# Turning rows by DMA instead of on TensorE, and a gated unit's new state in three GpSimd operations

## The chip, the cores and the metric

The kernel runs on one core of a Trainium2 chip. The metric is the device time of one execution in microseconds (us). The kernel before took 2233.61 us, the median of three runs (2232.93 to 2242.04).

The core's engines run side by side, each through its own queue in order, and wait for one another through semaphores: PE (TensorE, the matrix unit), DVE (VectorE), ACT (ScalarE), POOL (GpSimd) and SP, which here only issues DMAs. GpSimd issues DMAs too. SBUF is the on-chip memory of 128 partitions; PSUM is the smaller memory into which PE writes.[...]

## The reference

There are 16 graphs of 1024 nodes with 128 features each and a dense 0/1 adjacency matrix. Layer 0 runs four steps of a gated unit over each graph, layer 1 thins the adjacency matrix row by row ("skipping" below) and runs three graph layers over the thinned one. Cut to what matters here:

```python
# layer 0, four times, h = x at first
hw = h @ weight[i];  m = adj.T @ hw
gx = m @ w_ih.T + b_ih;  gh = h @ w_hh.T + b_hh
r = sigmoid(xr + hr);  z = sigmoid(xz + hz);  n = tanh(xn + r * hn)
h = (1 - z) * n + z * h

# layer 1, skipping: for each row n in order
num = row.sum();  sf = (num + 1) // 2 if num > 10 else 1
rm = row & (cumsum(row) % sf == 0)          # only if num > 1 and the node counts
carry[n] = row & ~rm                        # the row loses these entries ...
carry[:, n] = carry[:, n] & ~rm             # ... and so does column n of all rows
```

What row n removes, entry j, is also taken from row j at column n. So a later row needs, of every earlier row, the entry at its own place: a column of what the earlier rows left, which has to be turned into a row.

## The kernel before

The kernel has two stages. In the first, the gated unit (class Gated) and the skipping (class FixPoint) run together; in the second (class Sage), the three graph layers. A slower general path follows under a condition that the inputs don't meet.

**The gated unit.** Two streams take the graphs in turn, so that a layer of one stream runs while the other's state is turned and prepared. There are 64 layers of this kind (16 graphs, four steps), and each treats its 1024 nodes in two halves f of 512 columns. The state h of a stream is one SBUF tile of 128 features by 1024 nodes (`st.ht`). In `layer`, L1096 multiplies with the adjacency matrix, L1108 is every gate matmul, L1118 the sigmoid of r, L1121 and L1123 add the parts of n on DVE, L1124 is the tanh (written into the tile r) and L1127 the sigmoid of z. Then the new state is made as z * h - (z - 1) * n: L1131 (first half) or L1135 (second half) makes z * h on GpSimd, L1136 makes (z - 1) * n on DVE, and L1137 subtracts on GpSimd. The loop of L1133 does this for both halves after the gates of both. In the very last layer DVE does GpSimd's part too. Reading the new state begins a layer later, when the other stream's gates run: `turn` (L1041) turns one half after the other.

**The skipping.** A block is 128 rows, number k of a graph, for four graphs g at once; 32 blocks follow each other, k from 0 to 7 for graphs 0 to 3, then for 4 to 7, and so on. A block first masks its rows with what earlier blocks left: `read_back` (L715) reads, for k of 2 and more, the columns of this block from all blocks but the last one, out of DRAM (`not_r`, profile name e_nr), one DMA per graph on SP's queue, into one of four buffers f_rt; the part from the last block is still in SBUF (`fresh`, f_nr). `turn` (L726) transposes each 128x128 square on PE into one PSUM bank (`tr`, f_tr), `keep` (L731) masks the rows from there in one DVE operation over 128k columns, and `count` (L739) is a scan along the rows. Then the removals inside the block are settled, and `rows` (L870, L872) makes what is left of each row and stores it with L873. `check` of the gated unit (L1992) looks over a tile h_test that SP loads (L998).

**The order.** In this stage every engine's order is that of the program. `steps` is a generator with a yield between pieces; `layer` calls `aside(n)` at ten places, and each takes one piece, so a block of the skipping goes with exactly two layers of the gated unit. The masks of graphs 0 to 3 stand at places 6 and 8 of one layer and 2 and 4 of the next; `rows` at 2 to 4 of a block's later layer; the reads for the next block are issued at place 3, between the third and the fourth mask. The DMA queue of SP holds, in order, the four stores of L873, the four reads of L715 and the load of h_test. A read may start when its buffer is free and the stores it reads from have landed.

Of the kernel before, what the change touches and what calls it, by code (L numbers as in the profile page):

```python
# [8 lines left out]
F32 = mybir.dt.float32  # L9
BF = mybir.dt.bfloat16  # L10
# [4 lines left out]
AF = mybir.ActivationFunctionType  # L15
ALU = mybir.AluOpType
# [5 lines left out]
P = 128  # L22
B = 16
N = 1024
C = 128
NB = N // P
HF = 512
L0 = 4
# [602 lines left out]
class FixPoint:  # L631
# [76 lines left out]
    def read_back(self, i, g):  # L708

        if i >= len(self.todo) or self.todo[i][0] < 2:  # L710
            return
        k, b0 = self.todo[i]
        k1 = k - 1
        rt = self.rts.tile([P, NB - 2, P], BF, name="f_rt")
        self.nc.sync.dma_start(rt[:, :k1, :], self.not_r[b0 + g, :k1 * P, k * P:k * P + P]  # L715
                               .rearrange("(j p) n -> p j n", p=P))
        self.left[i, g] = rt

    def turn(self, i, g):

        k = self.todo[i][0]
        if k:
            rt = self.left.pop((i, g), None)
            for j in range(k):
                src = rt[:, j, :] if j < k - 1 else self.fresh[g][:, k * P:k * P + P]
                self.nc.tensor.transpose(self.tr[:, j, :], src, self.cst["ident_b"])  # L726

    def keep(self, i, a):
        k = self.todo[i][0]
        if k:  # L730
            self.nc.vector.scalar_tensor_tensor(a[:, :k * P], self.tr[:, :k, :].rearrange("p k n -> p (k n)"),  # L731
                                                0.0, a[:, :k * P], op0=ALU.is_ge, op1=ALU.mult)

    def count(self, i, g, a, rank, other):
        nc = self.nc
# [6 lines left out]
    def steps(self):  # L742

        nc, G = self.nc, self.G
        for c in range(G):
            self.load(c)
        old = None
        for i, (k, b0) in enumerate(self.todo):
            diag = slice(k * P, k * P + P)

            yield
            if old:
                old.settle()
                old.wide_u(0)
            yield
            if old:
                old.wide_u(1)
                old.rows(0)
            yield
            if old:  # L760
                old.wide_u(2)
                old.rows(1)
            yield
            if old:
                old.rows(2)
                old.wide_u(3)
                old.rows(3)
            a = [self.loaded.pop((i, g)) for g in range(G)]
            pt = self.ps.tile([P, G, P], F32, name="f_pd")
            turned = pt.rearrange("p g n -> p (g n)").bitcast(BF)[:, :G * P].rearrange("p (g n) -> p g n", g=G)  # L770
            for g in range(G):
                nc.tensor.transpose(turned[:, g, :], a[g][:, diag], self.cst["ident_b"])
            yield
            if old:
                old.last_u()

            both = self.small.tile([P, G, P], BF, name="f_both")
            for g in range(G):
                nc.vector.tensor_mul(both[:, g, :], a[g][:, diag], turned[:, g, :])
            nc.gpsimd.affine_select(both, both, pattern=[[0, G], [1, P]], compare_op=ALU.is_gt, fill=0.0,  # L780
                                    base=0, channel_multiplier=-1)
            self.turn(i, 0)
            yield
            rank = self.two.tile([P, G, N], F16, name="f_rank")
            self.keep(i, a[0])
            self.count(i, 0, a[0], rank, pt)
            yield
            yield
            self.turn(i, 1)
            self.keep(i, a[1])  # L790
            yield
            self.count(i, 1, a[1], rank, pt)
            if i == 0:

                for c in range(G, self.LOTS):
                    self.load(c)
            yield
            yield
            yield
            self.turn(i, 2)  # L800
            self.keep(i, a[2])
            self.count(i, 2, a[2], rank, pt)
            yield
            for g in range(G):
                self.read_back(i + 1, g)
            yield
            self.turn(i, 3)
            self.keep(i, a[3])
            self.count(i, 3, a[3], rank, pt)

            num = self.sm[:, 0, 0, :]
            nc.vector.tensor_scalar(num, rank[:, :, N - 1], 1.0, None, op0=ALU.mult)
            q = self.params(num, 0)
            u = self.diag_u(rank[:, :, diag], q)
            if old:
                old.check()
                for g in range(G):
                    self.load(G * (i - 1) + g + self.LOTS)
            yield
            x = self.removed(u, q, both)  # L820
            yield
            yield
            pd, num = self.less(x, rank, 1)
            rd = self.small.tile([P, G, P], F16, name="f_rd")
            q = self.params(num, 1, lambda: nc.vector.tensor_sub(rd, rank[:, :, diag], pd))
            u = self.diag_u(rd, q)
            yield
            x = self.removed(u, q, both)
            yield
            old = self.Block(self, i, a, rank, both, x)  # L830
            yield
        yield
        old.settle()
        for n in range(4):
            old.wide_u(n)
            if n < 3:
                yield
            old.rows(n)
        yield
        old.last_u()  # L840
        yield
        old.check()
# [81 lines left out]
class Gated:  # L924
# [7 lines left out]
    def __init__(self, ctx, tc, cst, x, adj, weight, w_ih, w_hh, b_ih, b_hh, summed, bad):  # L932
        self.tc, self.nc, self.cst = tc, tc.nc, cst
        self.x, self.adj, self.summed, self.bad = x, adj, summed, bad
        nc = self.nc
        pool = lambda name, **k: ctx.enter_context(tc.tile_pool(name=name, **k))
        self.adjp = pool("h_adj", bufs=NB)
        self.one = pool("h_one", bufs=1)
        self.wk = pool("h_wk", bufs=2)

        self.ps6 = pool("h_ps6", bufs=6, space=PSUM)
        self.wi = self.one.tile([C, L0, 3, C], F32, name="h_wi")
        self.wh = self.one.tile([C, L0, 3, C], F32, name="h_wh")
        self.bi = self.one.tile([C, L0 * 3], F32, name="h_bi")
        self.bh = self.one.tile([C, L0 * 3], F32, name="h_bh")
        self.bs = self.one.tile([C, L0 * 3], F32, name="h_bs")
        self.given = weight, w_ih, w_hh, b_ih, b_hh

    def bank(self):
# [20 lines left out]
    def prepare(self):  # L970
        nc, ident = self.nc, self.cst["ident"]
# [17 lines left out]
        for t, dst in zip(self.b_in, (self.bi, self.bh)):  # L989
            pt = bank()  # L990
            nc.tensor.transpose(pt[:, :L0 * 3], t, ident[:L0 * 3, :L0 * 3])
            nc.vector.tensor_copy(dst, pt[:, :L0 * 3])
        nc.vector.tensor_add(self.bs, self.bi, self.bh)

    def load_test(self, n):
        if n < B * 2:
# [81 lines left out]
    def layer(self, st, l, aside):  # L1078

        nc, wk = self.nc, self.wk  # L1080

        aid = nc.vector if (st.b, l) == (B - 1, L0 - 1) else nc.gpsimd
# [19 lines left out]
        bias = lambda t, g: t[:, 3 * l + g:3 * l + g + 1]  # L1102
# [5 lines left out]
                nc.tensor.matmul(pg, lhs, rhs, start=(i == 0), stop=(i == len(mm) - 1))  # L1108
            return pg

        rest = []
        for f in range(2):
            h, m = st.ht[:, half[f]], ms[f]
            r = wk.tile([C, HF], F32, name="h_r")
            z = wk.tile([C, HF], F32, name="h_z")
            zh = wk.tile([C, HF], F32, name="h_zh")
            pr = gate((w(self.wh, 0), h), (w(self.wi, 0), m))
            nc.scalar.activation(r, pr, AF.Sigmoid, bias=bias(self.bs, 0))  # L1118
            aside(5 + 2 * f)
            ph = gate((w(self.wh, 2), h))  # L1120
            nc.vector.scalar_tensor_tensor(r, ph, bias(self.bh, 2), r, op0=ALU.add, op1=ALU.mult)  # L1121
            px = gate((w(self.wi, 2), m))
            nc.vector.tensor_add(r, px, r)  # L1123
            nc.scalar.activation(r, r, AF.Tanh, bias=bias(self.bi, 2))  # L1124
            aside("rest" if f == 0 else 8)
            pz = gate((w(self.wh, 1), h), (w(self.wi, 1), m))
            nc.scalar.activation(z, pz, AF.Sigmoid, bias=bias(self.bs, 1))  # L1127

            rest.append((r, z, zh, h))
            if f == 0:  # L1130
                aid.tensor_tensor(zh, z, h, ALU.mult)  # L1131
                aside(6)
        for f, (r, z, zh, h) in enumerate(rest):  # L1133
            if f == 1:
                aid.tensor_tensor(zh, z, h, ALU.mult)  # L1135
            nc.vector.scalar_tensor_tensor(r, z, 1.0, r, op0=ALU.subtract, op1=ALU.mult)  # L1136
            aid.tensor_tensor(h, zh, r, ALU.subtract)  # L1137
        aside(9)

    def run(self, steps):  # L1140
# [937 lines left out]
```

## Time and profile before

| what | before |
|---|---|
| median of three runs | 2233.61 us |
| profiled execution, whole | 2232.83 us |
| its span, first to last instruction | 2230.8 us |
| PE, DVE, ACT, POOL busy | 2129.7, 1926.9, 1327.2, 1082.6 us |
| joint stage (about 40 to 1310 us), from 40 to 1270 us: PE, DVE, POOL busy | 1223.90, 1156.59, 596.79 of 1230 us |
| L726, transposes of f_rt and of f_nr | 336 and 112 |
| L731, masks | 112 |
| L1136 on DVE | 128, 99.1 us |
| L1131, L1135, L1137 on POOL | 63, 63 and 126; 80.1, 81.3 and 205.3 us |

Rows of the profile name line, engine, operation, written tile "<-" read tiles, shapes and how many; then busy time and mean, or, in order of time, the start and the length in us. "PEld" is the load of a matmul's stationary operand, which overlaps matmuls. The end of a matmul is modelled, so for PE the distance between starts tells more than the length. Bracketed text is idle time of the engine and what ended it.

### The profile page before, as it was taken

What the parts mean: (1) busy time and instruction counts of PE and PEld (TensorE: products, weight loads), DVE (VectorE), ACT (ScalarE), POOL (GpSimd) and SP (SyncE); (2) the same over time, 40 slices, a digit from 0 to 9 for tenths busy, and PEclk for the clock granted to TensorE, in tenths of its full rate; (3) what the DMA queues carried; (4) which work ended last, traced back from release to release, by engine and by line L of the source; (5) the groups of instructions that cost most, each with busy time, mean ns of one, the idle gap of its engine ahead of it and who ended that gap; (6) DMA issues with size and microseconds to landing.
All of it is one profiled execution on the core that took longest, in us unless ns stands there. A gap on an engine that the chain in (4) does not pass through costs nothing. (4 is left out here: it accounts for less than half of the span.)

```text
span 2230.8 us, 33341 instructions
## 1 busy us (share of the span) xinstructions
PE 2129.7 (95%) x10665; PEld 1456.6 (65%) x10665; DVE 1926.9 (86%) x4338; ACT 1327.2 (59%) x3238; POOL 1082.6 (49%) x1092
## 2 busy tenths in 40 slices
PE   6999999999999999999999979999999899998987
PEld 4566655666656666555665557777777678887865
DVE  4999999999998999999999978888888766666877
ACT  3657557565565656556566465666666455556756
POOL 4347437356355364364463346777777344551002
PEclk9999999999999999999999989999999999999989
DMA  8247347347356265364383259888888577765404
GB/s 251 71 103 240 80 114 229 71 120 214 86 156 177 73 200 138 90 201 118 73 264 85 64 184 329 305 305 297 305 301 304 169 259 260 257 221 174 152 29 144
DMA packets 214396, 402.46 MB, mean 180 GB/s; under 512 B 59586, under 2 KB 80740, under 8 KB 214212
## 3 DMA queue, kind: packets, MB, share of 16 engines
q1 hardware_dynamic: 168388, 280.68, 37.3%
q0 software_dynamic: 41472, 117.46, 19.3%
q10 hardware_dynamic: 4352, 2.11, 0.4%
q8 instruction: 86, 1.41, 0.3%
q14 instruction: 98, 0.80, 0.1%
HBM read 324.49 MB, written 109.25 MB: 194 GB/s over the span
## 5 line engine op out<-in xcount | busy, mean ns | idle before, releaser
L1108 PE MATMUL h_g<-h_h,h_wh 128*128 128x512 f32 x768 | 399.2, 601 | 3.1 <-DVE h_r L1121 3.1
L1108 PE MATMUL h_g<-h_ms,h_wi 128*128 128x512 f32 x768 | 392.1, 592 | 0.0
L739 DVE TENSOR_TENSOR_SCAN f_rank<-f_a,f_first,f_pd 128x1024 f16<-128x1024 bf16 x128 | 299.2, 2343 | 3.3
L1137 POOL TENSOR_TENSOR h_h<-h_zh,h_r 128x512 f32<-128x512 f32 x126 | 205.3, 1629 | 195.2 <-DVE h_r L1136 172.2
L1096 PE MATMUL h_g<-h_a,h_hi 128*128 128x512 f32 x1024 | 282.8, 417 | 2.2 <-DMA h_a<-in_adj_dram 2.0
L1108 PEld LDWEIGHTS h_g<-h_ms,h_wi 128*128 128x128 f32 x768 | 145.6, 190 | 183.9 <-issue 166.8
L1096 PE MATMUL h_g<-h_a,h_lo 128*128 128x512 f32 x1024 | 264.1, 395 | 0.0
L1513 POOL CAST p_b<-p_at 128x512 uint8<-128x512 f32 x256 | 219.4, 879 | 84.2 <-DVE p_at L1505 59.8
L1096 PEld LDWEIGHTS h_g<-h_a,h_hi 128*128 128x128 f32 x1024 | 188.4, 188 | 63.8 <-issue 20.1
L1096 PEld LDWEIGHTS h_g<-h_a,h_lo 128*128 128x128 f32 x1024 | 190.0, 188 | 39.4
L1406 ACT ACTIVATE s_junk<-s_o 128x128 bf16<-128x128 f32 x384 | 114.0, 298 | 170.7 <-DVE s_o L1399 170.7
L1131 POOL TENSOR_TENSOR h_zh<-h_z,h_h 128x512 f32<-128x512 f32 x63 | 80.1, 1271 | 275.5 <-ACT h_z L1127 275.5
L1108 PEld LDWEIGHTS h_g<-h_h,h_wh 128*128 128x128 f32 x768 | 129.2, 190 | 85.9 <-issue 65.5
L1099 ACT COPY h_ms<-h_g 128x512 f32<-128x512 f32 x128 | 73.8, 577 | 183.3 <-PE h_g L1096 139.3
L1124 ACT ACTIVATE h_r<-h_r,h_bi 128x512 f32<-128x512 f32 x128 | 92.3, 721 | 131.2 <-DVE h_r L1123 131.1
L916 ACT ACTIVATE f_u<-f_rank,f_q 128x128 f16<-128x128 f16 (+7 forms) x128 | 110.6, 867 | 74.9 <-DVE f_rank L856 74.9
L1992 DVE SCALAR_TENSOR_TENSOR p_junk<-p_a 128x1024 bf16<-128x1024 f32 x96 | 125.7, 1309 | 0.0
L893 ACT ACTIVATE f_pd<-f_rank,f_q 128x128 f32<-128x128 f16 x128 | 59.1, 461 | 109.8 <-DVE f_q L701 106.6
L1781 PE MATMUL q_ob<-s_wxp,q_xt 128*128 128x256 f32 x512 | 123.4, 385 | 0.3
L1505 DVE SCALAR_TENSOR_TENSOR p_at<-p_nr,p_u 128x128 fp32r<-128x128 bf16 (+1 forms) x192 | 102.5, 543 | 20.5 <-ACT p_at L1497 15.0
L1492 PE MATMUL p_u<-ident_b,p_nr 128*128 128x128 bf16 x1024 | 97.2, 224 | 7.2 <-DVE p_at L1505 5.0
L1423 POOL TENSOR_TENSOR q_rl<-s_r,q_rh 128x512 fp32r<-128x512 f32 x32 | 41.1, 1285 | 128.0 <-ACT q_rh L1422 105.5
(260 smaller groups left out, 4946.3 us busy)
## 6 DMA issues: line engine op xcount, KB each, us to landing
h_a<-in_adj_dram POOLq DMA_DIRECT2D x128, 512.0 KB, 9.5
p_a<-in_adj_dram SPq DMA_DIRECT2D x96, 512.0 KB
f_a<-in_adj_dram POOLq DMA_DIRECT2D x128, 256.0 KB, 6.6
e_nr<-f_nr SPq DMA_DIRECT2D x128, 256.0 KB
p_nr<-e_nr SPq DMA_DIRECT2D x32, 1024.0 KB
h_test<-in_adj_dram SPq DMA_DIRECT2D x32, 512.0 KB
s_at<-p_b SPq DMA_DIRECT2D x32, 512.0 KB
s_ag<-s_ag SPq DMA_DIRECT2D x64, 256.0 KB
```

The costliest lines, as they stand in the source:

```text
L739: nc.vector.tensor_tensor_scan(out, a, other[:, 0, 0:1].to_broadcast([P, N]), start, op0=ALU.add, op1=ALU.bypass)
L916: nc.scalar.activation(u[:, :n1], rank[:, g, :n1], AF.Abs, bias=q[:, 1, g:g + 1], scale=q[:, 0, g:g + 1])
L1096: nc.tensor.matmul(pm[f], part[:, j, :], st.adj[j][:, half[f]], start=(j == 0 and n == 0), stop=(j == NB - 1 and n == 1))
L1108: nc.tensor.matmul(pg, lhs, rhs, start=(i == 0), stop=(i == len(mm) - 1))
L1124: nc.scalar.activation(r, r, AF.Tanh, bias=bias(self.bi, 2))
L1137: aid.tensor_tensor(h, zh, r, ALU.subtract)
L1406: self.nc.scalar.activation(junk, o[:, i, :], AF.Square, accum_out=ss[:, i:i + 1])
L1492: nc.tensor.matmul(pu[:, i * P:(i + 1) * P], v[:, 4 * f + i, j * P:(j + 1) * P], self.cst["ident_b"], start=True, stop=True)
L1505: self.nc.vector.scalar_tensor_tensor(g["at"][:, j, c0:c0 + low], v[:, j, c0:c0 + low], 0.0, pu[:, :low], op0=ALU.is_lt, op1=ALU.is_lt)
L1513: self.nc.gpsimd.tensor_copy(g["b", f][:, j, :], g["at"][:, j, f * HF:(f + 1) * HF].bitcast(F32))
L1781: nc.tensor.matmul(pb[:, i], g["xt"][:, f, blk], self.wxp, start=(i % 2 == 0), stop=False)
L1992: nc.vector.scalar_tensor_tensor(junk, a, 0.0, a, op0=ALU.is_gt, op1=ALU.not_equal, accum_out=bad[:, c:c + 1])
```

## The change

Two things change. The columns of older rows are read from DRAM by a DMA that transposes them on the way, so that PE turns only the square from the last block; the mask is then two DVE operations where k is over 1, one on the DMA's tile in SBUF and one on PE's square in PSUM, and each graph g has its own square of `tr`. And the new state is h + (1 - z) * (n - h): ACT gives 1 - z as the sigmoid of the negated sum (a scale of -1 and a negated bias, made once by a small DVE operation), and GpSimd does a subtraction, a product and a sum, for each half right after that half's gates; DVE's L1136 goes. In the last layer DVE does these three.

```diff
 def read_back(self, i, g):
-        rt = self.rts.tile([P, NB - 2, P], BF, name="f_rt")
-        self.nc.sync.dma_start(rt[:, :k1, :], self.not_r[b0 + g, :k1 * P, k * P:k * P + P]
-                               .rearrange("(j p) n -> p j n", p=P))
+        rt = self.rts.tile([P, (NB - 2) * P], BF, name="f_rt")
+        self.nc.sync.dma_start(rt[:, :k1 * P], self.not_r[b0 + g, :k1 * P, k * P:k * P + P], transpose=True)
         self.left[i, g] = rt

     def turn(self, i, g):
         k = self.todo[i][0]
         if k:
-            rt = self.left.pop((i, g), None)
-            for j in range(k):
-                src = rt[:, j, :] if j < k - 1 else self.fresh[g][:, k * P:k * P + P]
-                self.nc.tensor.transpose(self.tr[:, j, :], src, self.cst["ident_b"])
-
-    def keep(self, i, a):
-        k = self.todo[i][0]
+            self.nc.tensor.transpose(self.tr[:, g, :], self.fresh[g][:, k * P:k * P + P], self.cst["ident_b"])
+
+    def keep(self, i, g, a):
+        k, stt = self.todo[i][0], self.nc.vector.scalar_tensor_tensor
         if k:
-            self.nc.vector.scalar_tensor_tensor(a[:, :k * P], self.tr[:, :k, :].rearrange("p k n -> p (k n)"),
-                                                0.0, a[:, :k * P], op0=ALU.is_ge, op1=ALU.mult)
+            last = slice((k - 1) * P, k * P)
+            if k > 1:
+                rt = self.left.pop((i, g))
+                stt(a[:, :(k - 1) * P], rt[:, :(k - 1) * P], 0.0, a[:, :(k - 1) * P], op0=ALU.is_ge, op1=ALU.mult)
+            stt(a[:, last], self.tr[:, g, :], 0.0, a[:, last], op0=ALU.is_ge, op1=ALU.mult)
...
+        self.bn = self.one.tile([C, L0 * 3], F32, name="h_bn")
...
+        nc.vector.tensor_scalar(self.bn, self.bs, -1.0, None, op0=ALU.mult)
...
-        rest = []
         for f in range(2):
...
-            zh = wk.tile([C, HF], F32, name="h_zh")
+            d = wk.tile([C, HF], F32, name="h_zh")
...
             pz = gate((w(self.wh, 1), h), (w(self.wi, 1), m))
-            nc.scalar.activation(z, pz, AF.Sigmoid, bias=bias(self.bs, 1))
-
-            rest.append((r, z, zh, h))
+            nc.scalar.activation(z, pz, AF.Sigmoid, bias=bias(self.bn, 1), scale=-1.0)
+            aid.tensor_tensor(d, r, h, ALU.subtract)
+            aid.tensor_tensor(d, z, d, ALU.mult)
+            aid.tensor_tensor(h, h, d, ALU.add)
             if f == 0:
-                aid.tensor_tensor(zh, z, h, ALU.mult)
                 aside(6)
-        for f, (r, z, zh, h) in enumerate(rest):
-            if f == 1:
-                aid.tensor_tensor(zh, z, h, ALU.mult)
-            nc.vector.scalar_tensor_tensor(r, z, 1.0, r, op0=ALU.subtract, op1=ALU.mult)
-            aid.tensor_tensor(h, zh, r, ALU.subtract)
         aside(9)
```

The calls of `keep` in `steps` pass the graph's number; nothing else changes.

More of the change, by code (lines that the diff above doesn't have):

```diff
@@ L784, in steps @@
             rank = self.two.tile([P, G, N], F16, name="f_rank")
-            self.keep(i, a[0])
+            self.keep(i, 0, a[0])
             self.count(i, 0, a[0], rank, pt)
@@ L789, in steps @@
             self.turn(i, 1)
-            self.keep(i, a[1])
+            self.keep(i, 1, a[1])
             yield
@@ L800, in steps @@
             self.turn(i, 2)
-            self.keep(i, a[2])
+            self.keep(i, 2, a[2])
             self.count(i, 2, a[2], rank, pt)
@@ L807, in steps @@
             self.turn(i, 3)
-            self.keep(i, a[3])
+            self.keep(i, 3, a[3])
             self.count(i, 3, a[3], rank, pt)
```

## The prediction

> **What bounds the kernel now.** I read the page's engine table first, then the busy times by stretch, then the order of time on TensorE around one block, and last VectorE and GpSimd side by side. The change touches only the joint stage, in which the layers of the gated unit and the blocks of the skipping run interleaved; by stretch it lasts from about 40 to 1310 us.
>
> The row below is that stage from 40 to 1270 us; columns are length, then busy time of PE, PEld, DVE, ACT and POOL.
>
> ```profile
> 40.00:1270.00 1230.00, 1223.90 (x4893) 744.04 (x4893) 1156.59 (x2332) 735.64 (x1369) 596.79 (x596) 1.00 0.48 136
> ```
>
> TensorE is busy for 99.5% of the stage at full clock, VectorE for 94%, GpSimd for 49%. A busy share alone can hide pauses, so I looked at the starts. PE alone, in order of time, in the block k = 6 of the third group of graphs, at the mask of its second graph:
>
> ```profile
> 902.51 0.44 PE L726 MATMUL f_tr<-ident_b,f_rt 128*128 128x128 bf16 x5
> 902.79 0.22 PE L726 MATMUL f_tr<-ident_b,f_nr 128*128 128x128 bf16 x1
> 902.85 1.08 PE L1108 MATMUL h_g<-h_h,h_wh 128*128 128x512 f32 x2
> 903.76 1.02 PE L1108 MATMUL h_g<-h_ms,h_wi 128*128 128x512 f32 x2
> ```
>
> Five turns take 0.28 us from start to start, the sixth 0.06, and then the gate matmuls go on at 0.43 us each. Nothing waits. TensorE's queue sets the length of this stage, and what leaves it is gained; VectorE stands right behind it (77.3 of 80 us busy from 240 to 320 us), so it has to be counted too.
>
> **What the Trainium skill says.** "GPSIMD Engine Reference", section "Specifications", says GpSimd's SBUF interfaces are shared with VectorE, with contention for VectorE instructions in a two-port mode or with two SBUF inputs. The trace agrees, in two forms (order of time, VectorE and GpSimd):
>
> ```profile
> 348.41 3.91 DVE L1136 SCALAR_TENSOR_TENSOR h_r<-h_z,h_r 128x512 f32<-128x512 f32 x2
> 348.62 1.28 POOL L1131 TENSOR_TENSOR h_zh<-h_z,h_h 128x512 f32<-128x512 f32 x1
> 349.87 1.29 POOL L1074 TENSOR_TENSOR h_x<-h_x,h_w 128x512 f32<-128x512 f32 x1
> ...
> 930.37 1.64 DVE L1992 SCALAR_TENSOR_TENSOR h_junk<-h_test 128x1024 bf16<-128x1024 f32 x1
> 931.01 2.14 POOL L1137 TENSOR_TENSOR h_h<-h_zh,h_r 128x512 f32<-128x512 f32 x1
> 931.94 1.50 DVE L870 TENSOR_SCALAR f_w<-f_u,f_q 128x1024 bf16<-128x1024 f16 x1
> ```
>
> In the first three lines VectorE's two-input operation started while GpSimd worked, and was held until GpSimd's back-to-back operations were over (3.91 us for the pair; 1.28 at 927.24). In the last three L1992 slipped in between two GpSimd operations, the second of which then took 2.14 us instead of 1.29, and L870 waited for that one (1.50 us; its median is 0.48). VectorE operations with an input in PSUM show no such hold: L1123 takes 692 to 694 ns wherever it falls.
>
> For the transposing DMA no row of this trace exists. "VectorE: DVE Perf Modes", section "The three transpose paths", prices one 128x128 bf16 transpose by DMA at 1309 ns; "DMA: Bandwidth & Descriptors", section "Latency and other measured facts", gives 261 GB/s for such a DMA with non-contiguous source. These are my two ends.
>
> **The change, part by part.**
>
> 1. Turns on TensorE. 336 transposes of older rows go (4 x (1+2+3+4+5+6) per group of four graphs, four groups); the 112 of fresh rows stay. Runs of five at 902.51, 908.30 and 912.39 us took 0.28 to 0.29 us, so 57 ns each: 336 x 0.057 = 19.2 us, on the path that sets the end. An upper value: the blocks that turn two and six rows per graph, in the same layer l, last 38.73 and 39.97 us between rows of L812 (400.4 to 439.1, 558.8 to 598.8), which makes 1.24/16 = 0.078 us and 26 us in all; part of that is VectorE's longer masking. I take 19.2.
>
> 2. The masking on VectorE. L731 reads 128k columns from PSUM (0.28 us for 128, 0.133 more per further 128). Now for k > 1 it is one operation with both inputs in SBUF and one of 128 columns from PSUM: one more fixed part of about 0.15 us (0.28 - 0.13), 96 times, 14 us. L886 (both inputs in SBUF, 512 columns, median 0.69) shows the same rate as L731 with 512 (0.68), so I expect no faster mode.
>
> 3. L1136 leaves VectorE: 126 x 0.68 = 86 us without its holds, 99 with them. For the last layer VectorE did six operations after the gates and does six again.
>
> 4. GpSimd: 252 operations (63 of L1131, 63 of L1135, 126 of L1137; 80.1 + 81.3 + 205.3 = 367 us) become 378, at 1.27 to 1.29 us each as L1131 and L1135 show when not held, 486 us, so busy time rises from 597 to about 715 of 1230 us. In place or not makes no difference that L1074 would show (median 1.28). They depend on each other, and dependent ones leave a gap of about 0.08 us (L1135 ends at 930.93, L1137 starts at 931.01), so a chain takes about 4.0 us. The first half's chain now runs before the second half's gates end, in time that GpSimd spent waiting (L1131 waited 275.5 us for z). The second half's new h was there 4.5 to 5.8 us after its z (709.49 to 713.99, 729.00 to 734.77), through two VectorE and three GpSimd operations; now three GpSimd operations give 4.0. The next reader, the turn of that half in the other stream's layer, comes 13 us after z (722.57). So this costs nothing; without that cover it would cost a microsecond or two per layer. GpSimd's DMA issues stand behind the same number of operations at a layer's end as before.
>
> 5. Where the holds fall. At 900 us the first mask starts at 900.32, tanh ends at 900.56; the second at 905.60 and 905.84. The subtraction needs only tanh, so each mask is ahead of GpSimd by about 0.3 us and not held. The third mask, behind a scan that ends near 909.0, meets the second chain (906.4 to 910.3) and waits up to 1.3 us. The fourth meets DMA issues alone. The first L870 of a block waited 1.0 us for L1137 and will start after the chain: gain 1.0. L1992 may wait 0.8 more. Per block: -2.56 (two pairs of L1136) - 1.0 + 0.6 + 1.3 + 0.8 = -0.9 us for VectorE, against -0.6 for TensorE (19.2/32). VectorE stays just behind TensorE and doesn't take over.
>
> 6. The transposing DMAs, issued from SP. Each waits until the mask of the block before has read its buffer, about 2 us later than now, when it waits for the turn. Here is SP's queue at 858 us:
>
> ```profile
> 858.84 14.47 SPq L715 DMA_DIRECT2D f_rt<-e_nr  x4
> 873.37 0.52 SPq L998 DMA_DIRECT2D h_test<-in_adj_dram  x1
> ```
>
> Each read is used one block, some 38 us, later, and h_test, queued behind them, about 17 us later (in the next block, issued at 913.28 and read by L1992 at 930.37). The stores of L873 stand 35 us behind the first. At 261 GB/s the longest (192 KB) takes 0.75 us; at 1309 ns per square, one after another, 4 x 6 x 1.309 = 31 us, from 901.1 to 932.5, and with 2.5 us for h_test's 512 KB, estimated from 128 packets of 4 KB at 0.18 us, the trace's mean for them, on 16 engines, plus 1.1 us from issue to first packet as plain f_rt reads show, L1992 would come some 5 us late in each of four blocks, 0.3 us in four others. I take the value of full cover, nothing: the 1309 ns must hold the fixed latency of one DMA, and plain reads of the same 256-byte rows landed within a few us.
>
> 7. L994's operation on 12 columns, before the first block: nothing, since the first gate comes later. ACT's z has another sign and bias, not another duration (0.67).
>
> Sum: span 2230.8 - 19.2 = 2211.6; the profiled execution took 2232.83, 2.0 more than its span, and the median is 0.8 above that: 2214 us. About 0.5% (11 us) is what a measurement of this kernel can tell from no change.
>
> **Rivals.**
>
> A, the forecast: 2204 to 2224, chance 0.57.
>
> B, VectorE takes over. The lead of 0.3 us of the first two masks is thin; if both lose it, each waits for one GpSimd operation, +2.6 us per block with k > 1. VectorE then ends 1.7 us per such block above today, 24 x 1.7 = 41 us, of which today's 73 us of idle time absorb perhaps half; the freed TensorE time turns into waits of L1108 and L1096 for VectorE. Time 2226 to 2244. For: VectorE's 96% in late blocks. Against: the order of starts above. Chance 0.17.
>
> C, slower: the transposing DMAs come late. They share SP's queue and h_test stands behind them; VectorE then stops at L1992, and TensorE with it. With r us per 128x128 in series, lateness is 24r - 26 us in the blocks before k = 7 and 20r - 26 before k = 6, four of each. At r = 1.31 the loss is about 23 us and eats the gain; above r = 1.35 the kernel is slower than before by over 0.5%; at r = 1.6 it is 74 us, so 2289; at 2.0 over 160. For: no row of this trace shows such a DMA, and rows of 256 bytes are short. Against: 38 us of cover. Chance 0.20.
>
> D, more: with VectorE relieved TensorE's small pauses go too, at 0.078 us per turn and more, 2192 to 2204. Chance 0.06.
>
> **How the numbers follow.** A and D are faster: 0.63. B is mostly no change: 0.16. C and a corner of B are slower: 0.21. The range from 2200 to 2252 holds A, B, most of D's upper half and C's mildest part, about 0.8. A's own range is 2204 to 2224.
>
> **What would show it.** Right: L726 with 112 turns; stage ends about 19 us earlier with PE still near 99%; L1131, L1136 and L1137 gone, 378 GpSimd operations near 1.3 us; L870's mean near 0.5 us; no idle time before the mask that ends with a DMA of f_rt. Wrong, by B: masks from SBUF that take over 1 us longer than their width says, and PE idle on VectorE. Wrong, by C: VectorE idle before the masks or L1992 that ends with a DMA, and long rows of L715 on SP's queue.

## The result and the profile after

The changed kernel takes 2216.23 us, the median of four runs (2210.52 to 2218.72), beside 2236.76 us for the kernel before on the same chip (2232.93 to 2242.04): a ratio of 0.991, with a 95% interval from 0.9896 to 0.9923. That is 20.5 us less; 2214 had been predicted. The profiled execution took 2210.52 us with a span of 2208.8, 22.0 less than before. The row sums of the last block come 20.7 us earlier (L811 at 1256.1 us, L812 of before at 1276.8), so nearly all of it lies in the joint stage.

The engine table of the page, kernel after; busy time, share of the span and instructions of each engine:

```profile
PE 2106.5 (95%) x10329; PEld 1436.6 (65%) x10329; DVE 1850.3 (84%) x4309; ACT 1326.4 (60%) x3238; POOL 1228.3 (56%) x1218
```

The 336 matmuls are gone (10665 before), GpSimd has 126 operations more, and VectorE is busy 76.6 us less. Over the stretch from 40 to 1270 us that the prediction showed, the busy times (length, then PE, PEld, DVE, ACT, POOL) are:

```profile
40.00:1270.00 1230.00, 1221.77 (x4635) 736.63 (x4634) 1099.98 (x2351) 744.87 (x1387) 747.84 (x726) 1.00 0.49 136
```

PE reads 99.3%, after 99.5% before. VectorE went from 1156.59 to 1099.98 us, 4.6 points of its share, and GpSimd from 596.79 to 747.84. The stretch is fixed in time, so the changed kernel gets more of its work done in it; between the first and the last row sums of each kernel, which is the same work, VectorE's busy time fell from 1159.5 to 1084.2 us. The groups of GpSimd's new chain, from the page (count, busy time and mean in ns, idle time before them):

```profile
L1128 POOL TENSOR_TENSOR h_zh<-h_r,h_h 128x512 f32<-128x512 f32 x126 | 169.9, 1348 | 279.3 <-ACT h_r L1124 276.1
L1129 POOL TENSOR_TENSOR h_zh<-h_z,h_zh 128x512 f32<-128x512 f32 x126 | 165.3, 1312 | 9.9
L1130 POOL TENSOR_TENSOR h_h<-h_h,h_zh 128x512 f32<-128x512 f32 x126 | 174.8, 1387 | 9.9
```

They are the 378 operations of step 4, at 1.31 to 1.39 us: 510 us where 486 were expected. VectorE's groups that the change touches, joint stage, kernel after:

```profile
L871 DVE TENSOR_TENSOR f_nr<-f_w,f_a 128x1024 bf16<-128x1024 bf16 x124 | 92.5, 746 | 4.3
L869 DVE TENSOR_SCALAR f_w<-f_u,f_q 128x1024 bf16<-128x1024 f16 x124 | 75.1, 606 | 18.1 <-ACT f_u L918 17.8
L730 DVE SCALAR_TENSOR_TENSOR f_a<-f_rt,f_a 128x128 bf16<-128x128 bf16 (+5 forms) x96 | 62.9, 655 | 0.0
L1987 DVE SCALAR_TENSOR_TENSOR h_junk<-h_test 128x1024 bf16<-128x1024 f32 x31 | 58.2, 1878 | 0.0
L731 DVE SCALAR_TENSOR_TENSOR f_a<-f_tr,f_a 128x128 bf16<-128x128 bf16 x112 | 31.9, 285 | 15.9 <-PE f_tr L722 15.9
```

The same groups, kernel before:

```profile
L1136 DVE SCALAR_TENSOR_TENSOR h_r<-h_z,h_r 128x512 f32<-128x512 f32 x124 | 96.5, 813 | 3.7 <-ACT h_z L1127 3.7
L870 DVE TENSOR_SCALAR f_w<-f_u,f_q 128x1024 bf16<-128x1024 f16 x124 | 91.4, 737 | 6.5 <-ACT f_u L919 5.9
L872 DVE TENSOR_TENSOR f_nr<-f_w,f_a 128x1024 bf16<-128x1024 bf16 x124 | 85.9, 693 | 4.3
L731 DVE SCALAR_TENSOR_TENSOR f_a<-f_tr,f_a 128x128 bf16<-128x128 bf16 (+6 forms) x112 | 75.9, 678 | 9.8 <-PE f_tr L726 9.7
L1992 DVE SCALAR_TENSOR_TENSOR h_junk<-h_test 128x1024 bf16<-128x1024 f32 x31 | 55.7, 1797 | 0.0
```

L1136 is gone (-96.5), L870's successor is 16.3 us shorter, the masks are 18.9 longer (62.9 + 31.9 against 75.9), the product 6.6 longer and the look at h_test 2.5: together 84.8 us less, 2.7 us per block. A sixth group, L899 (L900 before) on f_u and f_both, both in SBUF, grew by 5.1 us, so that VectorE as a whole has 76.6 us less, 2.4 per block. No mask from f_rt has idle time before it, so none waited for a transposing DMA.

Now the race between masks and GpSimd. In order of time, the k = 6 block of the third group, kernel after (start, length; in brackets idle time and what ended it):

```profile
888.22 0.82 DVE L730 SCALAR_TENSOR_TENSOR f_a<-f_rt,f_a 128x640 bf16<-128x640 bf16 x1
888.37 0.67 ACT L1127 ACTIVATE h_z<-h_g,h_bn 128x512 f32<-128x512 f32 x1
888.54 1.62 POOL L1128 TENSOR_TENSOR h_zh<-h_r,h_h 128x512 f32<-128x512 f32 x1 [1.58 <-ACT h_r L1124]
...
890.24 1.27 POOL L1129 TENSOR_TENSOR h_zh<-h_z,h_zh 128x512 f32<-128x512 f32 x1
891.59 1.28 POOL L1130 TENSOR_TENSOR h_h<-h_h,h_zh 128x512 f32<-128x512 f32 x1
```

The mask starts 0.32 us ahead of GpSimd, takes its plain 0.82 us, and GpSimd's first operation is the one that gets longer, 1.62 us. In all blocks the masks from f_rt were held for about 4 us altogether, all of it where k = 4.

### The profile page after: what moved, and what is told of

Its sections match the earlier page's. It is cut to its first block, busy times and chain, and to the rows that moved or that the text cites. A ratio compares the mean times of both kernels' runs of the same rounds, so it can differ in the third digit from the quotient of the medians.

```text
span 2208.8 us, 33036 instructions
## 1 busy us (share of the span) xinstructions
PE 2106.5 (95%) x10329; PEld 1436.6 (65%) x10329; DVE 1850.3 (84%) x4309; ACT 1326.4 (60%) x3238; POOL 1228.3 (56%) x1218
## 5 line engine op out<-in xcount | busy, mean ns | idle before, releaser
L1128 POOL TENSOR_TENSOR h_zh<-h_r,h_h 128x512 f32<-128x512 f32 x126 | 169.9, 1348 | 279.3 <-ACT h_r L1124 276.1
L1508 POOL CAST p_b<-p_at 128x512 uint8<-128x512 f32 x256 | 218.4, 875 | 84.8 <-DVE p_at L1500 58.4
L1130 POOL TENSOR_TENSOR h_h<-h_h,h_zh 128x512 f32<-128x512 f32 x126 | 174.8, 1387 | 9.9
L1129 POOL TENSOR_TENSOR h_zh<-h_z,h_zh 128x512 f32<-128x512 f32 x126 | 165.3, 1312 | 9.9
L892 ACT ACTIVATE f_pd<-f_rank,f_q 128x128 f32<-128x128 f16 x128 | 59.1, 462 | 101.6 <-DVE f_q L701 98.5
```

What stands on the lines that cost most here:

```text
L1128: aid.tensor_tensor(d, r, h, ALU.subtract)
L1129: aid.tensor_tensor(d, z, d, ALU.mult)
L1130: aid.tensor_tensor(h, h, d, ALU.add)
L1508: self.nc.gpsimd.tensor_copy(g["b", f][:, j, :], g["at"][:, j, f * HF:(f + 1) * HF].bitcast(F32))
```

## Experiments

T was the theory of the prediction: TensorE sets the stage, and its 336 turns are the gain. V was the rival: VectorE sets it, together with TensorE, and the operation that left VectorE is the gain. L, in the later expectations, is what the first runs left standing: the two set the stage together, and a cut pays where it is made on both. All ratios below are to the kernel before on the same chip, with 95% intervals.

**Each half alone.** e1 has the skipping of the changed kernel with the old code for the new state (L1136 still on VectorE, and the loop over both halves as before). e2 has the old skipping (its reads, all turns on PE, one mask operation) with the new state:

```diff
 # e1, against the changed kernel
-            aid.tensor_tensor(d, r, h, ALU.subtract)
-            aid.tensor_tensor(d, z, d, ALU.mult)
-            aid.tensor_tensor(h, h, d, ALU.add)
+            rest.append((r, z, zh, h))
...
 # e2, against the changed kernel
-            self.nc.tensor.transpose(self.tr[:, g, :], self.fresh[g][:, k * P:k * P + P], self.cst["ident_b"])
+            for j in range(k):
+                src = rt[:, j, :] if j < k - 1 else self.fresh[g][:, k * P:k * P + P]
+                self.nc.tensor.transpose(self.tr[:, j, :], src, self.cst["ident_b"])
```

> Only the older rows turned by DMA; the new state as in the kernel before (L1131, L1135 and L1137 on GpSimd, L1136 on VectorE). Theory T (TensorE's queue sets the joint stage, each turn costs it 57 ns): TensorE is relieved of 19.2 us, VectorE gets 14 us of split masks and no relief, so most of the gain comes but VectorE's 73 us of idle time get tight: 10 to 17 us faster than before, ratio 0.9925 to 0.9955. Theory V (VectorE paces, and the changed kernel gains because L1136 left it): no gain or a loss, ratio 1.000 to 1.006.

> Only the new state in three GpSimd operations; all 448 turns stay on TensorE and the mask is one VectorE operation from PSUM. Theory T: TensorE has the same work, only its small pauses shrink: 0 to 5 us faster, ratio 0.998 to 1.000. Theory V: VectorE loses 86 to 99 us of work, so 15 us or more faster, ratio 0.985 to 0.993.

Measured: e1 2243.99 us, ratio 1.0034 (1.0023 to 1.0046); e2 2225.65 us, 0.9951 (0.9936 to 0.9966). Taking the turns off TensorE, by itself, makes the kernel slower, as V had it; taking L1136 off VectorE, by itself, gives about half of the gain, which lies between the ranges of T and V. Added up, the two alone would make 0.9985; together they make 0.991. Neither half explains the result without the other.

Where e1 loses is seen in order of time, in the k = 4 block of its third group, on VectorE, GpSimd and PE (in e1 the mask is L730, the new state L1130):

```profile
824.64 6.71 DVE L730 SCALAR_TENSOR_TENSOR f_a<-f_rt,f_a 128x384 bf16<-128x384 bf16 x1
824.77 1.28 POOL L1073 TENSOR_TENSOR h_x<-h_x,h_w 128x512 f32<-128x512 f32 x1
826.01 2.48 POOL L1060 TENSOR_TENSOR h_lo<-h_x,h_hi 128x512 fp32r<-128x512 f32 x2
828.46 1.25 POOL L1130 TENSOR_TENSOR h_zh<-h_z,h_h 128x512 f32<-128x512 f32 x1
829.68 1.25 POOL L1073 TENSOR_TENSOR h_x<-h_x,h_w 128x512 f32<-128x512 f32 x1
...
831.60 0.27 PE L722 MATMUL f_tr<-ident_b,f_nr 128*128 128x128 bf16 x1 [4.34 <-DVE f_a L731]
```

A mask whose plain length is 0.55 us took 6.71, until a whole run of GpSimd operations had passed, and TensorE, whose next turn needed the bank that the mask pair reads, stood still for 4.34 us. This is the extreme, and it came once: in the other three groups this mask took 0.55 us and the next one 1.25 to 1.26. A smaller loss comes in every third block or so. In order of time in the k = 7 block of the same group, e1, VectorE, ACT and PE:

```profile
970.43 0.16 DVE L701 SCALAR_TENSOR_TENSOR f_q<-f_tr,f_t 128x4 f32<-128x4 f32 x1
...
970.63 1.95 ACT L892 ACTIVATE f_pd<-f_rank,f_q 128x128 f32<-128x128 f16 x4 [5.83 <-DVE f_q L701]
...
972.51 0.67 ACT L1117 ACTIVATE h_r<-h_g,h_bs 128x512 f32<-128x512 f32 x1
...
973.32 0.63 PE L1040 MATMUL h_g<-ident,h_h 128*128 128x128 f32 x4 [1.71 <-ACT h_r L1117]
```

VectorE, late, gives late what it derives from the row sums (L701); ACT, in its own order, waits 5.83 us for it with L892 and does the sigmoid of r only afterwards; that sigmoid frees the PSUM bank that TensorE needs next. VectorE's lateness so reaches TensorE through ACT's queue. The idle time of that one PE line (the fp32 turns of the state) is a gauge for it, here in the joint stage of the kernel before, after and in e1:

```profile
L1041 PE MATMUL h_g<-ident,h_h 128*128 128x128 f32 x488 | 73.5, 273 | 0.1
L1042 PE MATMUL h_g<-ident,h_h 128*128 128x128 f32 x492 | 74.2, 273 | 1.9 <-ACT h_r L1118 1.8
L1040 PE MATMUL h_g<-ident,h_h 128*128 128x128 f32 x480 | 72.5, 274 | 13.3 <-ACT h_r L1117 13.3
```

The 13.3 us of e1 are 11 waits of 0.6 to 1.7 us, in the last three blocks of the groups, and before each of them ACT had waited 4.7 to 6.0 us for L701. They are a part of what e1 loses: all waits of TensorE that the trace marks make 27 us between the first and the last row sums of e1, 6 in the kernel before.

**The turns given back.** The changed kernel, with as many turns on TensorE as were taken away (e3), and twice as many (e9). They go to a square of `tr` that nobody reads; e9 has `range(2 * (k - 1))`, from the columns j % 8:

```diff
             self.nc.tensor.transpose(self.tr[:, g, :], self.fresh[g][:, k * P:k * P + P], self.cst["ident_b"])
+            for j in range(k - 1):
+                self.nc.tensor.transpose(self.tr[:, 4, :], self.fresh[g][:, j * P:j * P + P], self.cst["ident_b"])
```

> The changed kernel with 336 further transposes on TensorE at the places where the older rows were turned, into a square of PSUM that nobody reads. They add no work to VectorE or to a DMA. Theory T: 336 x 57 ns = 19 us come back, ratio to before 0.998 to 1.001. Theory V: TensorE has room, at most 3 us come back, ratio 0.991 to 0.9925.

> As e3, with 672 instead of 336 further transposes on TensorE, 38 us of work by 57 ns each. e3 brought about 4 to 5 us of 19 back. Theory L (two queues in lockstep; the changed kernel has some TensorE slack in late blocks, which the first 336 used up): the second 336 cost nearly their full 19 us, so 18 to 25 us above the changed kernel, ratio 0.998 to 1.002. If TensorE had room all along: 10 us or less above it, ratio below 0.995.

Measured: e3 2218.98 us, 0.9927 (0.9912 to 0.9941); e9 2238.44 us, 1.0016 (1.0005 to 1.0026). The changed kernel stands at 0.991, and at 0.9903 when run again (e5, below). So the first 336 turns cost some 4 to 5 us of the 19 that T gave them (each ratio is good to about 3 us); the second 336 cost 0.0089, 20 us, their full length. In the changed kernel TensorE has room for most of the turns that were taken away, and no more than that.

**VectorE's work given back.** The changed kernel with one more VectorE operation per half, on z, after the gates, of about L1136's length (0.68 us, 88 us in all), whose result nobody reads (e8), beside the changed kernel again (e5):

```diff
+            zs.append(z)
...
+        for z in zs:
+            nc.vector.bn_stats(wk.tile([C, 6], F32, name="h_fill"), z)
```

> The changed kernel as it is, for comparison on the same chip: ratio 0.990 to 0.992 by every theory.

> The changed kernel with one statistics operation of VectorE over z (128 x 512, one input, 0.69 us, its result unused) per half, where L1136 stood: 128 x 0.69 = 88 us of work on VectorE, none on another engine, and not of a kind that GpSimd holds. Theory L: VectorE paces again, 15 to 25 us above the changed kernel, ratio 0.998 to 1.003. Theory T: VectorE has room, at most 5 us above, ratio 0.991 to 0.9935.

Measured: e5 2212.95 us, 0.9903 (0.9886 to 0.9919); e8 2241.45 us, 1.0028 (1.0017 to 1.0039). With the 336 turns still off TensorE, VectorE's 88 us cost 28.5 us, more than the whole gain and a little more than the 15 to 25 that L expected. The gauge line, groups of e8 in the joint stage:

```profile
L1042 PE MATMUL h_g<-ident,h_h 128*128 128x128 f32 x488 | 73.9, 274 | 15.7 <-ACT h_r L1119 15.7
```

15.7 us, by the same way through ACT as in e1: again 11 waits, each behind a wait of ACT for L701. What T could not have is here plain: this kernel has less work on TensorE than the kernel before, and is slower. The run settles one thing more. The new state stands earlier than before in e8 too, and the gain is gone, so the shorter chain to the new state doesn't bring it by itself; the work has to leave VectorE.

**TensorE's work against its time.** To put these runs on one scale, I took from each trace the time between the first and the last of the 32 row sums (L812 of before; 31 blocks), and priced all matmuls that start in it by the distance between starts when they follow each other without a wait: 0.429 us for a gate matmul, 0.229 for one with the adjacency matrix, 0.109 for an fp32 turn, 0.057 for a bf16 square. The rest is pauses. In us:

| kernel | time | TensorE's work | pauses |
|---|---|---|---|
| before | 1232.9 | 1207.9 | 25.2 |
| e1, turns by DMA alone | 1246.0 | 1190.4 | 55.8 |
| e2, new state alone | 1222.0 | 1207.4 | 14.7 |
| e3, after with the turns back | 1220.3 | 1206.6 | 13.7 |
| after | 1212.9 | 1188.7 | 24.2 |
| e8, after with VectorE's work back | 1236.0 | 1190.4 | 45.8 |
| e9, after with twice the turns | 1236.6 | 1225.7 | 10.9 |
| e7, below | 1203.9 | 1177.4 | 26.4 |

Some 11 us of pauses remain even where TensorE clearly sets the pace (e9). What lies above that is time in which something else was last, and in the kernel before that was 14 us, in a stage whose profile calls PE 99.5% busy. (The same 336 turns make 19.2 us of work in one pair of rows and 17.5 in another, as the stretch cuts the matmuls at its ends differently.)

Each row is one traced execution, and that of e1 was the longest of its twelve (2252.19 us, where the median is 2243.99), so its pauses are on the high side. Some of them are not pauses either. TensorE's granted clock was full in this stage in all rows but two: in e1 it was 0.5 for 3.4 us from 649.5 us and for 6.8 us from 830.4, in e7 for 3.4 us from 824.1. Each time TensorE had just stood still, or was still doing so (for 1.7, 4.34 and 2.1 us). In that stretch of e1 gate matmuls follow each other at 0.85 us instead of 0.43, which makes about 5 us of e1's 55.8 (an estimate, half of 10.2 us). If the falls belong to the pauses, as their places suggest, a wait for VectorE costs TensorE more than its own length.

Compare e1 with before: 17.5 us of work left TensorE and 30.6 us of pauses came. Compare e2 with before: no work left TensorE, and 10.5 us of pauses went. Only both together take the work away and keep the pauses where they were.

**Are the transposing DMAs hidden?** e4 reads every square twice by a transposing DMA, the second time into a buffer that nobody uses:

```diff
+        r2 = self.rts.tile([P, (NB - 2) * P], BF, name="f_rt2", bufs=2)
+        self.nc.sync.dma_start(r2[:, :k1 * P], self.not_r[b0 + g, :k1 * P, k * P:k * P + P], transpose=True)
```

> The changed kernel with every transposing read issued twice, the second into two spare buffers that nobody reads (the second of a buffer waits for the landing of an earlier one). Theory T (the reads lie under 38 us of cover): within 2 us of the changed kernel, ratio 0.990 to 0.992. Theory C (the reads are near the end of their cover, SP's queue and h_test behind them): 10 us or more longer than the changed kernel, ratio above 0.995, with VectorE idle before L730 or before the look at h_test on account of a DMA.

Measured: 2218.88 us, 0.9925 (0.9911 to 0.9939), 3 to 5 us above the changed kernel (0.991 and 0.9903), with intervals that overlap; that is just above T's range and below C's. Twice the DMAs cost no more than that, and no mask waited for one. Rival C falls. SP's queue of the kernel after, at the block shown above, explains why nothing was late:

```profile
889.06 13.29 SPq L715 DMA_TRANSPOSE f_rt<-e_nr  x4
902.41 0.91 SPq L999 DMA_DIRECT2D h_test<-in_adj_dram  x1
```

The four reads and the load behind them are through the queue within 14.3 us, where the plain ones of the prediction's view took 15.1, and the reads are used a block later.

**Does the order of the two masks matter?** In the changed kernel the mask from f_rt stands ahead of the one that waits for TensorE. e10 swaps them:

```diff
+            stt(a[:, last], self.tr[:, g, :], 0.0, a[:, last], op0=ALU.is_ge, op1=ALU.mult)
             if k > 1:
                 rt = self.left.pop((i, g))
                 stt(a[:, :(k - 1) * P], rt[:, :(k - 1) * P], 0.0, a[:, :(k - 1) * P], op0=ALU.is_ge, op1=ALU.mult)
-            stt(a[:, last], self.tr[:, g, :], 0.0, a[:, last], op0=ALU.is_ge, op1=ALU.mult)
```

> The changed kernel with the two masks of a graph in the other order: first the square from PSUM, which waits for TensorE's turn, then the columns from the DMA's tile. Theory L: VectorE waits for each turn again, and the two-input mask now starts 0.28 us later, at the moment of GpSimd's first subtraction, where before it had 0.3 us of lead, so the first or second mask of a group is held up to 1.3 us: 5 to 15 us above the changed kernel, ratio 0.9925 to 0.997, and L730's counterpart 1 us longer than its width says in many blocks. If neither the order nor the lead matters: within 3 us, ratio 0.9895 to 0.992.

Measured: 2216.58 us, 0.992 (0.9903 to 0.9937). More masks were held; the group with k = 4, e10:

```profile
L731 DVE SCALAR_TENSOR_TENSOR f_a<-f_rt,f_a 128x384 bf16<-128x384 bf16 x16 | 19.2, 1203 | 0.0
```

Its mean is 1203 ns where the plain length is 0.55 us, and where k is 2 or 3 one mask of four was held too; about 18 us of holds in all. The kernel's time moved by 2 to 4 us, which the intervals don't tell from none and which lies at the upper end of what was expected if neither order nor lead matters. So rival B's step (lost leads mean lost time) is weaker than I had priced it, as long as L1136 is gone.

**Further along the same road.** If both engines set the pace, work must leave both. e6 turns the rows from the last block by DMA too, out of SBUF, so that one mask operation is left; e7 also turns three of the four squares on the diagonal by DMA:

```diff
 # rows
-            fix.fresh[g] = nr
+            k1 = self.k + 1
+            if k1 < NB:
+                rt = fix.left[self.i + 1, g]
+                nc.sync.dma_start(rt[:, self.k * P:k1 * P], nr[:, k1 * P:k1 * P + P], transpose=True)
...
 # keep: one operation
+            stt(a[:, :k * P], rt[:, :k * P], 0.0, a[:, :k * P], op0=ALU.is_ge, op1=ALU.mult)
...
 # e7, start of a block
+            for g in range(1, G):
+                nc.sync.dma_start(dg[:, g, :], self.loaded[i, g][:, diag], transpose=True)
```

> The changed kernel with the square of the last block turned by a DMA too, from SBUF (f_nr) into the same tile as the older rows, behind the store of that row on SP's queue; TensorE makes no turn of rows, and the mask is one VectorE operation with both inputs in SBUF. Removes 112 x 57 ns = 6.4 us from TensorE and 96 x 0.15 = 14 us from VectorE. Theory L (TensorE and VectorE set the joint stage together, and a cut pays where it is made on both): 5 to 10 us below the changed kernel, ratio 0.9865 to 0.989. Theory T (TensorE alone): 6 us below. If a turn from SBUF comes late, VectorE is idle before the masks on a DMA and the time is above the changed kernel's.

> As e6, and three of the four diagonal squares of a block (the turns of f_a into f_pd) by DMA from SBUF as well, issued at the block's start: 96 x 57 ns = 5.5 us more off TensorE, nothing off VectorE. Theory L: 0 to 4 us below e6, more of it in early blocks. Theory T: 5.5 us below e6. A loss if SP's queue, with 12 turns of 1.1 us in a block, delays the stores or reads.

Measured, on the same chip as e5: e6 2206.19 us, 0.9872 (0.9854 to 0.9889); e7 2203.62 us, 0.9858 (0.9842 to 0.9875), against 0.9903 (0.9886 to 0.9919) for the changed kernel. e7 beats both kernels, with some 32 us less than before and 9 less than the change. The 6.8 us between e5 and e6 fit L (5 to 10) and T (6) alike; the 2.6 us between e6 and e7 fit L (0 to 4) better than T (5.5), but the two intervals overlap. Masks from f_rt, groups of e7:

```profile
L728 DVE SCALAR_TENSOR_TENSOR f_a<-f_rt,f_a 128x512 bf16<-128x512 bf16 x16 | 15.2, 948 | 10.4 <-DMA f_rt<-f_nr 10.3
L728 DVE SCALAR_TENSOR_TENSOR f_a<-f_rt,f_a 128x384 bf16<-128x384 bf16 x16 | 9.1, 566 | 0.0
```

In these two, for the first time, masks do wait for a transposing DMA (10.3 us in all in e7), since the fresh rows are turned right before they are used.

**One more operation to GpSimd?** e11 is e6 with the product of the fourth graph (L871, one of four) on GpSimd, e12 is e7 with the same:

```diff
-            nc.vector.tensor_mul(nr, w, self.a[g])
+            (nc.gpsimd if g == 3 else nc.vector).tensor_tensor(nr, w, self.a[g], ALU.mult)
```

> As e6 (all row turns by DMA), and of the four products w * a of a block (L872 of the kernel before, 0.69 us each on VectorE) the fourth on GpSimd, which waits there for the next instruction anyway. Takes 32 x 0.69 = 22 us off VectorE, puts some 32 x 2.5 us (an estimate, from 1.3 us for 512 columns) on GpSimd. Theory L: VectorE still takes part in the pace, so 3 to 8 us below e6, ratio 0.9835 to 0.986. If GpSimd's later start of the next operations or a hold of VectorE's two-input operations eats it: e6 or above, ratio 0.987 or more.

> The same step on top of e7. There three of the products that follow on VectorE (L779 of the kernel before) have both inputs in SBUF, and may be held by GpSimd's product for up to 2.5 us in each block, so theory L expects less than in e11: between 4 us below and 10 us above e7, ratio 0.984 to 0.990, with those products over 1 us each time they are held.

Measured: e11 2207.55 us, 0.9865 (0.9846 to 0.9884), no different from e6, where L had expected 3 to 8 us less; e12 2243.36 us, 1.0036 (1.0023 to 1.0049), 40 us worse than e7, where L had expected at most 10. Groups of e11, then of e12:

```profile
L868 POOL TENSOR_TENSOR f_nr<-f_w,f_a 128x1024 bf16<-128x1024 bf16 x32 | 68.1, 2127 | 150.2 <-DVE f_w L866 150.2
L728 DVE SCALAR_TENSOR_TENSOR f_a<-f_rt,f_a 128x512 bf16<-128x512 bf16 x16 | 22.2, 1389 | 9.0 <-DMA f_rt<-f_nr 9.0
```

```profile
L776 DVE TENSOR_TENSOR f_both<-f_a,f_dg 128x128 bf16<-128x128 bf16 x92 | 74.8, 866 | 0.0
```

In e11 22 us of VectorE (32 products of 0.69) become 68 on GpSimd, and the mask at k = 4 takes 1.39 us, where e6 has 0.99. VectorE's busy time in the stage falls by 10 us only: what it gained comes back for more than half as longer operations with two SBUF inputs (the masks 7.4 us, L899 5.9). Why the rest gains nothing was not tried. The trace shows two masks of 4.9 us, TensorE standing still for 3.1 us some 20 us after each, and its granted clock at 0.5 for 3.4 us about then.

In e12 three small products of a block are fed from SBUF, as in e7 (0.22 us there). In 31 of the 32 blocks one of the three falls under GpSimd's long product and takes 2.15 us, which makes 60 us of holds and the mean of 0.87. TensorE's pauses on the scale above are 60 us, and its granted clock was 0.5 five times for 3.4 us. That this is the reason for the 40 us is read from these figures, and not tried apart.

## Why the prediction was right, and where not

The time, the sign and case A were right: 2216 against 2214. But the step that made the number was right by half, and that it came so close is in part luck.

**Step 1 failed in its reason.** The 336 turns did take 57 ns each off TensorE, and TensorE's work fell by 19.2 us (1207.9 to 1188.7). "On the path that sets the end ... what leaves it is gained" was wrong. Alone they gained nothing (e1, +7.6 us); beside the new state they are worth 4 to 11 us (0.991 and 0.9903 against e3's 0.9927 and e2's 0.9951). The mistake lies in the first part: matmuls that follow each other without a wait, at 902.51 us, were taken for the whole stage, and the busy share of 99.5% backed it up. I wrote that a busy share can hide pauses, looked at one place, and missed 25 us of them, 14 of which are more than e9 keeps. The Trainium skill, "Perfetto Trace Analysis", section "Identifying the Most-Contended Engine", says that a matmul's busy share is no good measure of how near TensorE is to its limit, since matmuls are pipelined; there it warns of instructions that look too small, here they looked too large: the five turns at 902.51 us are listed with 0.44 us and follow each other within 0.28.

**Step 5, VectorE's relief, was too small, and it was the other half.** I had -0.9 us per block and concluded that VectorE "stays just behind"; it measured -2.4 (76.6 us), of which the five groups above make -2.7. L1136 gave 96.5 us instead of 82 with its holds, and the charges were too high: 1.3 us per block for the third mask and 0.8 for L1992 make 67 us, of which 4 us of holds on masks and 2.5 us on L1992 came. The first L870 of a block gained 0.5 us per block, not 1.0 (its group's mean is 0.61 us, not 0.5), and the product behind it lost 0.2. Two errors met: too much credited to TensorE, too little to VectorE.

**Rival B** was sound in its worry and wrong in its cause. VectorE does bind, but the leads of the masks held as step 5 said (0.32 us at 888.22), and even where they are lost (e10) little follows. Its sentence that idle time on VectorE absorbs half of what is added has no fixed worth: in e1 VectorE's busy time grew by 10.5 us and the stage by 13.1, though TensorE had 17.5 us less to do, while in e8, with 129 us of idle time to begin with, 88 us put back cost 28.5. **Rival D** had the mechanism that e2 shows, pauses of TensorE that go when VectorE is relieved (10.5 us), but in the changed kernel, with the turns gone too, the pauses are back at 24.2 us.

**Steps that held.** Step 2: masks 18.9 us longer, with 14 from fixed parts expected and 4 of the rest holds. Step 3: L1136 left with all its 96 to 99 us. Step 4: 378 operations at 1.31 to 1.39 us; new h stood 3.5 us (first half) and 3.65 us (second) after z at the median, where 4.0 had been expected and the kernel before has 6.5 and 5.8. Step 6: the DMAs were hidden, and the 1309 ns that the Trainium skill ("VectorE: DVE Perf Modes", section "The three transpose paths") gives for one square don't add up from square to square: their packets of 256 bytes took 23.0 ns in the mean, those of the plain copies 19.2, and 128 of them on 16 engines make some 0.18 us per square (an estimate from the 23.0). The prediction's other end, 261 GB/s, is given by the page that it cites for a non-contiguous middle dimension, and no run here shows it.

**What stays open.** e3 is e2 with the mask cut in two and with transposing reads, and is no slower (0.9927 against 0.9951, with intervals that touch), though VectorE's operations add up to 12 us more. That its mask no longer waits for six turns may be why; e10 was to show it and moved too little to decide. Open too is why e11 gained nothing, and what lets the granted clock fall to 0.5: e8 had four pauses of 1.7 us without it, e1 and e12 one each of 1.7 and 1.6 us with it.

## What to carry to other kernels

When two in-order engines are both nearly full, a cut on one is worth little until the other is cut too: run each half of a change alone, and put the work back by halves, before one of them is given the credit. Judge TensorE by the distances between starts, summed over the whole stage and set against its time; the pauses that remain are the share of the others. And look for the way by which a late engine reaches the bound one: here it ran through the order of a third, ACT, that was only 60% busy.

## What the runs showed of the hardware

- A VectorE operation with two SBUF inputs was held not for one GpSimd operation but for a whole run without gaps: 6.71 us for five operations (e1, once), 3.9 to 4.2 us for three (e12, four masks of 0.68 us). The Trainium skill, "GPSIMD Engine Reference", section "Specifications", names the contention for such operations; that section says nothing of how long. Within the new chain, whose operations depend on each other, a gap of about 0.08 us let VectorE in, and the next GpSimd operation took 1.49 us instead of 1.27 (four times, k = 4); where the mask had started first, at 888.22 us, it was 1.62.
- A transposing DMA holds SP's queue 1.11 to 1.18 us per instruction (medians of the kernel after by number of squares, one to six, with no rise from one to six), a plain one of the same data 0.37. SP has room for it here.
- In a stage at full clock, pauses of TensorE of 3.1 us (e11, e12) and 4.34 us (e1) came with a granted clock of 0.5 for 3.4 and 6.8 us, in which gate matmuls followed each other at 0.85 us instead of 0.43.
- DMA turned squares within SBUF as well, 112 in e6 and 208 in e7, and the kernel got shorter by it (6.8 us from e5 to e6); for the fresh rows the turn came so late that masks waited 6.8 us in e6 and 10.3 in e7, all told.
- GpSimd takes 2.13 us for a bf16 product of 1024 columns, three times VectorE's 0.69.
